# Transposing x once: the first stage stores its transposed tokens, the third stage completes them with an accumulating transfer

## The chip, the cores and the metric

The kernel runs on one core of one Trainium2 chip. The metric is device time in microseconds (us) of the whole program, all in float32. A core has TensorE (matmul, PE in the profile), VectorE (DVE), ScalarE (ACT), GpSimd (POOL) and SyncE (SP, which here only issues transfers), and 16 DMA engines that carry out the transfers of all of them.

## The reference

The input x has 384 x 384 tokens of 128 channels. Two layers follow each other, both on this array; all weights are 128 x 128.

```python
# layer 0
z = layernorm(x) * norm_g + norm_b
left  = (z @ Wl + bl) * sigmoid(z @ Wlg + blg)
right = (z @ Wr + br) * sigmoid(z @ Wrg + brg)
core = einsum('ikh,jkh->ijh', left, right)
x1 = x + sigmoid(x @ Wg + bg) * (layernorm(core) * onorm_g + onorm_b) @ Wout + bout-terms
# layer 1
left = x1 @ (W_left + W_eq) + biases
right_sum = sum over j of (x1 @ W_right + b_right)
out = (left * right_sum * sigmoid(x1 @ W_gate + b_gate)) @ W_out + b_out
y = layernorm(out + x1)
```

The layer norms take mean and variance over the 128 channels of a token. The sum over k in `core` needs every token of layer 0 before any token of the output, which splits the kernel into stages.

## The kernel before, in words

**First stage (0 to about 1142 us).** It walks over 144 chunks: 128 values of k on the partitions, eight values of i (XR), 128 channels. A chunk is two steps of four tokens per partition. `load_chunk` brings x (L106). `stats` computes mean and variance on VectorE (L215, L217), six steps ahead. `powers` turns them into rs = (var + eps)^-0.5 and sh = 1 - mean * rs on GpSimd (L224 to L227). `scale` writes z = x * rs + sh, the normalized token plus one, on GpSimd (L235). The "plus one" lets the bias of the weights come in by the matmul: the columns of `wz` are made so that the added one gives the bias. `front` transposes four tokens on TensorE (L244) and copies them to SBUF as zt (L246). `back` multiplies zt with the 512 columns of `wz` (left, right and the two gates, L267), applies the sigmoid on ScalarE (L269, two tokens at once) and the product on VectorE (L271) into the tile lr. A lr tile gathers 64 values of i (16 steps). It is written to DRAM (`lr_d`) by `store_slice` in eight slices of 1 MB (L253), one per step, during the 16 steps that fill the next tile. There are 18 such groups; the last two stay in SBUF and are not stored.

Per step, TensorE has half of `back`, then the four transposes for the next step, then the other half. The order of the instructions on each engine is written out by hand (`seq` keeps it); what an instruction waits for follows from the tiles it uses. A pool with n buffers of a tile makes its n+1st use wait until the first is free. A transfer is issued by the engine named in the code and waits in that engine's order.

**Second stage (about 1142 to 1885 us).** For each of the 128 h it loads left and right (L86, L87), makes nine pairs of matmuls (L357) and writes `core` to DRAM (L371), with sums for the layer norm over h.

**Third stage (about 1885 us to the end).** One iteration of the loop over t works on one row i of 384 tokens, with the channels on the partitions. `front(f)` runs ahead of the rest, by 14 rows at first and later by two. It transposes x of row f (three transposes, L448, and a copy on ScalarE to xT, L450) and, for row f - 2, computes the gate of layer 0 from xT (L440, sigmoid L442). `scale_core` multiplies core with its inverse deviation on GpSimd (L464). `layer0` makes x1T: matmul L473, then two operations on VectorE (L474, L476, which adds xT). `gated_left` has L490, L491, L493, L495, `layer1` L502 and L503 (which transposes the row back to tokens), `stats1` and `norm1` the last layer norm, `last` scale and shift of it, and `store` writes four rows at once. x is loaded four rows at a time by `load_x` (L399), 16 rows ahead; `load_core` brings four rows of core (L404) and of the inverse deviation, sent to all 128 partitions alike (rt, L406), eight rows ahead. Four PSUM banks rotate among the matmul results pg, pxt, pr, pg2, pl and pq, four others hold py.

So x is transposed twice: in the first stage after the normalization, in the third stage as it is.

Of the kernel before, what the change touches and what calls it, by code (L numbers as in the profile page):

```python
# [8 lines left out]
F32 = mybir.dt.float32  # L9
AF = mybir.ActivationFunctionType  # L10
ALU = mybir.AluOpType
# [8 lines left out]
def triangle_then_gated_row_kernel(ctx: ExitStack, tc: tile.TileContext, a: dict, out: bass.AP):  # L20
# [6 lines left out]

    nc = tc.nc  # L30
    x = a["x"].rearrange("b i j c -> (b i) j c")
    y = out.rearrange("b i j c -> (b i) j c")
# [7 lines left out]
    KEEP = 2  # L40
    RG = 4
    A = 14

    cpool = ctx.enter_context(tc.tile_pool(name="const", bufs=1))
# [3 lines left out]
    rstd_d = dpool.tile([N, N], F32, name="rstd_d")  # L48

    def seq(ins):  # L50

        return tc.keep_in_program_order(ins)
# [21 lines left out]
    with ExitStack() as ctx2:  # L74
# [13 lines left out]
                loaded2[h] = t  # L88

        with tc.tile_pool(name="p1x", bufs=6, side="right") as xp, \  # L90
             tc.tile_pool(name="p1w", bufs=3, side="right") as wp, \
             tc.tile_pool(name="p1s", bufs=5, side="right") as sp, \
             tc.tile_pool(name="p1t", bufs=2, space=PSUM) as tps, \
             tc.tile_pool(name="p1p", bufs=3, space=PSUM) as pps:
            NQ = XR // 4
# [111 lines left out]
            def stats(n, q, half):  # L207

                if q == 0 and half == 0:
                    normed[n] = [sp.tile(s, F32, tag=t, name=t) for t, s in  # L210
                                 (("st", [P, XR, 6]), ("mv", [P, XR, 2]), ("rs", [P, XR]), ("sh", [P, XR]))]
                st, mv, rs, sh = normed[n]
                r0 = 4 * q + 2 * half
                for r in range(r0, r0 + 2):
                    seq(nc.vector.bn_stats(st[:, r, :], loaded[n][:, r, :]))  # L215
                for r in range(r0, r0 + 2):
                    seq(nc.vector.bn_aggr(mv[:, r, :], st[:, r, :]))  # L217

            def powers(n, q):


                if q == NQ - 1:
                    _, mv, rs, sh = normed[n]
                    seq(nc.gpsimd.tensor_scalar(rs, mv[:, :, 1], EPS, 1.0, ALU.add, ALU.mult))  # L224
                    seq(nc.gpsimd.tensor_tensor(rs, rs, mhalf[:, :XR], ALU.pow))
                    seq(nc.gpsimd.tensor_tensor(sh, mv[:, :, 0], rs, ALU.mult))
                    seq(nc.gpsimd.tensor_scalar(sh, sh, -1.0, 1.0, ALU.mult, ALU.add))  # L227

            def scale(n, q):

                xt, (_, _, rs, sh) = loaded[n], normed[n]
                z = wp.tile([P, 4, C], F32, tag="z", name="z")
                for r in range(4):
                    rr = 4 * q + r
                    seq(nc.gpsimd.tensor_scalar(  # L235
                        z[:, r, :], xt[:, rr, :], rs[:, rr:rr + 1], sh[:, rr:rr + 1], ALU.mult, ALU.add
                    ))
                return z

            def front(z):  # L240
# [6 lines left out]
                return zt  # L247

            def store_slice():

# [5 lines left out]
                        in_=t[:, hs:hs + HS].rearrange("k h i s -> k h (i s)"),  # L256
                    ))

            def back(n, q, zt, half):

                kb, ig, c = chunks[n]
                if c == 0 and q == 0 and half == 0:
                    lr[kb, ig] = lrp.tile([P, H, G, 2], F32, tag="lr", name="lr")
                t = lr[kb, ig]
                pr = pps.tile([P, 2, 4 * H], F32, tag="pr", name="pr")
                for r in range(2):
                    seq(nc.tensor.matmul(pr[:, r, :], lhsT=zt[:, 2 * half + r, :], rhs=wz, start=True, stop=True))  # L267
                sg = wp.tile([P, 2, 2 * H], F32, tag="sg", name="sg")
                seq(nc.scalar.activation(sg, pr[:, :, 2 * H:], AF.Sigmoid))  # L269
                i0 = c * XR + 4 * q + 2 * half  # L270
                seq(nc.vector.tensor_tensor(  # L271
                    t[:, :, i0:i0 + 2, :],
                    pr[:, :, :2 * H].rearrange("k i (h s) -> k h i s", s=2),
                    sg.rearrange("k i (h s) -> k h i s", s=2),
                    ALU.mult,
                ))
# [7 lines left out]
            zs = {}  # L284
            for k in range(AHEAD):
                for half in range(2):
                    stats(*steps[k], half)
                if k == 1:
                    fold()
                if k == 2:  # L290
                    weights()
                if k < AHEAD - 1:
                    powers(*steps[k])
                if k == 1:
                    zs = {j: scale(*steps[j]) for j in range(2)}
                    zt = front(zs.pop(0))
            for k, (n, q) in enumerate(steps):
                ahead = None
                if k + 2 < len(steps):
                    zs[k + 2] = scale(*steps[k + 2])  # L300
                if k + AHEAD - 1 < len(steps):
                    powers(*steps[k + AHEAD - 1])
                for half in range(2):
                    back(n, q, zt, half)
                    if half == 0 and k + 1 < len(steps):
                        ahead = front(zs.pop(k + 1))
                    if k + AHEAD < len(steps):
                        stats(*steps[k + AHEAD], half)
                zt = ahead
                if q == NQ - 1:  # L310
                    del loaded[n], normed[n]
                    load_chunk(n + 6)
                store_slice()
                if k == 4:
                    for t, src in later:
                        load(t, src)
                if k == 20:
                    late_weights()
                if k == len(steps) - 2 * G // 4 + 16:
                    assert not full  # L320
                    for h in range(3):
                        load_h(h)
# [54 lines left out]
    with ExitStack() as ctx3:  # L377
        def pool(name, bufs, **kw):
            return ctx3.enter_context(tc.tile_pool(name=name, bufs=bufs, reuse_waits="tile", **kw))

        xip, fp, inp, op = pool("p3x", 4), pool("p3f", A + 4), pool("p3in", 3), pool("p3out", 3)
        wp, lp, sp = pool("p3w", 4), pool("p3l", 7), pool("p3s", 4)
        ps, ps2 = pool("p3ps", 4, space=PSUM), pool("p3ps2", 4, space=PSUM)

        def bank(name):
# [8 lines left out]
        rows, yts, pair, quad, xin, cin = {}, {}, {}, {}, {}, {}  # L394

        def load_x(i0):
            if i0 < N:
                xt = xin[i0] = xip.tile([P, RG, NB, C], F32, tag="xt", name="xt")
                seq(nc.sync.dma_start(out=xt, in_=x[i0:i0 + RG].rearrange("i (b p) c -> p i b c", p=P)))  # L399

        def load_core(i0):
            if i0 < N:
# [32 lines left out]
        def front(f):  # L435
# [5 lines left out]
                gT = r["gT"] = work("gT", fp)  # L441
                seq(nc.scalar.activation(gT, pg[:, :N], AF.Sigmoid, bias=bg0))  # L442
            if f < N:
                if f % RG == 0:
                    load_x(f + 4 * RG)
                pxt = bank("pxt")
                for b, s in enumerate(cols):
                    seq(nc.tensor.transpose(pxt[:, s], xin[f // RG * RG][:, f % RG, b, :], ident))  # L448
                xT = work("xT", fp)
                seq(nc.scalar.copy(xT, pxt[:, :N]))  # L450
                rows[f] = {"xT": xT}

        def right_sums(m):
# [12 lines left out]
        def layer0(i):  # L466
# [5 lines left out]
            pr = bank("pr")  # L472
            seq(nc.tensor.matmul(pr[:, :N], lhsT=wc, rhs=r["cs"], start=True, stop=True))  # L473
            seq(nc.vector.scalar_tensor_tensor(pr[:, :N], pr[:, :N], bz, r["gT"], ALU.add, ALU.mult))  # L474
            x1T = r["x1T"] = work("x1T", lp)
# [10 lines left out]
        def gated_left(i):  # L486
# [7 lines left out]
            u = r["u"] = work("u", lp)  # L494
# [54 lines left out]

        for i0 in range(0, 4 * RG, RG):  # L550
            load_x(i0)
        f = 0
        for t in range(N + 3):

            while f < min(N + 2, t + max(2, A - t // 3)):
                if f == 6:
                    rstd()
                    load_core(0)
# [72 lines left out]
```

## Time and profile before

The median of three runs is 3442.92 us (3438.89 to 3443.39); the profiled run has a span of 3438.5 us and a mean granted TensorE clock of 0.996.

| | first stage, 500 to 900 us | second stage, 1420 to 1600 us | third stage, 2400 to 2800 us |
|---|---|---|---|
| PE busy | 400.00 of 400 us | 180.00 of 180 us | 400.00 of 400 us |
| DVE busy | 268.71 | 94.62 | 329.07 |
| ACT busy | 173.20 | 70.75 | 306.48 |
| POOL busy | 293.62 | 105.43 | 291.75 |
| DMA share | 0.69 | 0.92 | 0.61 |
| GB/s | 196 | 283 | 198 |

Busy time is the time in which an engine has an instruction in work; the ends of matmuls are modelled. The DMA share is the mean busy share of the 16 DMA engines; it can exceed 1 in a short window, since an engine can have more than one packet in work. A line of groups reads: line, engine, operation, output <- inputs, shapes, count | busy us, mean ns of one | idle time of the engine just before them and what ended it.

Durations of one instruction that matter for what is changed: the transposes L448 and L244 274 ns (128x128), the copy L450 475 ns (128x384), the copy L246 580 ns (128x512), L235 448 ns (128x128), L474 and L476 625 and 618 ns (128x384). Transfers: a slice of lr is 1024 KB and lands 9.7 us (median) after its issue, a load of x in the first stage 512 KB and 7.7 us, a load of x in the third stage 768 KB and 4.9 us, one of rt 768 KB and 7.8 us.

### The profile page before, as it was taken

What the parts mean: (1) busy time and instruction counts of PE and PEld (TensorE: products, weight loads), DVE (VectorE), ACT (ScalarE), POOL (GpSimd) and SP (SyncE); (2) the same over time, 40 slices, a digit from 0 to 9 for tenths busy, and PEclk for the clock granted to TensorE, in tenths of its full rate; (3) what the DMA queues carried; (4) which work ended last, traced back from release to release, by engine and by line L of the source; (5) the groups of instructions that cost most, each with busy time, mean ns of one, the idle gap of its engine ahead of it and who ended that gap; (6) DMA issues with size and microseconds to landing.
All of it is one profiled execution on the core that took longest, in us unless ns stands there. A gap on an engine that the chain in (4) does not pass through costs nothing.

```text
span 3438.5 us, 48057 instructions
## 1 busy us (share of the span) xinstructions
PE 3398.4 (99%) x13646; PEld 2104.5 (61%) x13646; DVE 2414.3 (70%) x7498; ACT 1946.0 (57%) x3815; POOL 2357.5 (69%) x4041
## 2 busy tenths in 40 slices
PE   8999999999999999999999999999999999999998
PEld 4444444444444566666665677777777777777775
DVE  6666666666666555555555788888888888888887
ACT  3344444444444333333334677777777777777776
POOL 6677777777777455555655577777777777777776
PEclk9999999999999999999999999999999999999999
DMA  4776867758765599999999665665656666565662
GB/s 109 202 214 178 232 190 202 227 166 229 199 192 157 175 284 285 284 281 282 282 284 276 209 215 193 202 203 191 213 185 209 196 199 206 188 213 188 206 215 85
DMA packets 884865, 726.00 MB, mean 211 GB/s; under 512 B 18533, under 2 KB 823017, under 8 KB 884601
## 3 DMA queue, kind: packets, MB, share of 16 engines
q1 hardware_dynamic: 878176, 718.22, 67.9%
q10 hardware_dynamic: 6232, 4.13, 0.4%
q8 instruction: 110, 1.80, 0.2%
q14 instruction: 155, 1.26, 0.1%
q0 software_dynamic: 192, 0.59, 0.0%
HBM read 437.07 MB, written 285.80 MB: 210 GB/s over the span
## 4 chain that ended last, share of the span: by engine, by line
PE 98%; ACT 1%; DVE 0%; issue 0%; POOL 0%; DMA 0%; POOLq 0%; SPq 0%; ACTq 0%; DVEq 0%
PE pr L267 29%; PE pc L357 22%; PE pr L473 7%; PE py L502 7%; PE pg L440 7%; PE pg L490 7%; PE pl L491 7%; PE pt L244 4%; PE pxt L448 4%; PE py L503 4%; ACT py L533 0%; PE pq L457 0%; DMA xt<-in_x_dram 0%; POOL rs L522 0%; ACT gT L442 0%
## 5 line engine op out<-in xcount | busy, mean ns | idle before, releaser
L267 PE MATMUL pr<-wz,zt 128*128 128x512 f32 x2304 | 1040.0, 594 | 0.7 <-ACT zt L246 0.7
L357 PE MATMUL pc<-rr,lrh 128*128 128x384 f32 x2304 | 743.3, 486 | 1.5 <-issue 1.5
L269 ACT ACTIVATE sg<-pr 128x512 f32<-128x512 f32 x576 | 344.2, 598 | 644.9 <-PE pr L267 331.6
L267 PEld LDWEIGHTS pr<-wz,zt 128*128 128x128 f32 x2304 | 416.3, 191 | 414.9 <-issue 413.8
L271 DVE TENSOR_TENSOR lr<-pr,sg 128x512 f32<-128x512 f32 x576 | 398.5, 692 | 376.1 <-ACT sg L269 376.1
L357 PEld LDWEIGHTS pc<-rr,lrh 128*128 128x128 f32 x2304 | 451.8, 196 | 293.2 <-issue 2.3
L533 ACT ACTIVATE py<-py,nm,rs 128x128 f32<-128x128 f32 x1152 | 495.2, 430 | 120.2 <-POOL rs L526 89.8
L235 POOL TENSOR_SCALAR z<-xt,rs,sh 128x128 f32<-128x128 f32 x1152 | 497.7, 448 | 0.6 <-POOL z L235 0.4
L502 PEld LDWEIGHTS py<-wo,u 128*128 128x128 f32 x2304 | 377.5, 191 | 102.4 <-ACT wo L484 1.7
L366 DVE TENSOR_TENSOR csum<-csum,ct 128x1152 f32<-128x1152 f32 x128 | 184.8, 1444 | 351.1 <-ACT ct L363 351.1
L502 PE MATMUL py<-wo,u 128*128 128x128 f32 x2304 | 403.0, 275 | 1.2 <-ACT wo L484 1.2
L363 ACT COPY ct<-pc 128x1152 f32<-128x1152 f32 x128 | 143.3, 1119 | 450.1 <-PE pc L357 450.1
L343 POOL COPY rr<-lrh 128x768 f32<-128x768 f32 x128 | 184.5, 1442 | 307.6 <-DMA lrh<-lr_d 294.3
L464 POOL TENSOR_TENSOR cs<-ct,rt 128x384 f32<-128x384 f32 x384 | 383.3, 999 | 7.3 <-PE pr L473 5.4
L545 POOL TENSOR_TENSOR yt<-yt,lnb 128x384 f32<-128x384 f32 x384 | 383.8, 1000 | 2.9 <-DVE yt L544 2.7
L517 DVE BATCH_NORM_STATS2 st<-py 128x6 f32<-128x128 f32 x1152 | 266.7, 287 | 110.9 <-PE py L503 110.9
L473 PE MATMUL pr<-cs,wc 128*128 128x384 f32 x768 | 319.3, 497 | 0.7 <-ACT xT L450 0.7
L440 PE MATMUL pg<-xT,mat_L_conv_Wg 128*128 128x384 f32 x768 | 313.7, 490 | 4.7 <-ACT xT L450 4.7
L474 DVE SCALAR_TENSOR_TENSOR pr<-pr,bz,gT 128x384 f32<-128x384 f32 x384 | 240.2, 625 | 110.3 <-PE pr L473 110.3
L493 ACT ACTIVATE g<-pg,col_L_conv_b_gate 128x384 f32<-128x384 f32 x384 | 223.1, 581 | 162.2 <-PE pg L490 162.1
L503 PE MATMUL py<-ident,x1T 128*128 128x128 f32 x1152 | 314.0, 273 | 0.0
L490 PE MATMUL pg<-x1T,mat_L_conv_W_gate 128*128 128x384 f32 x768 | 310.9, 487 | 2.0 <-ACT gT L442 1.4
(88 smaller groups left out, 5125.8 us busy)
## 6 DMA issues: line engine op xcount, KB each, us to landing
lr_d<-lr SPq DMA_DIRECT2D x128, 1024.0 KB, 9.7
lrh<-lr_d SPq DMA_DIRECT2D x128, 768.0 KB, 7.7
xt<-in_x_dram SPq DMA_DIRECT2D x96, 768.0 KB, 4.9
ct<-core_d SPq DMA_DIRECT2D x96, 768.0 KB, 6.6
rt<-rstd_d SPq DMA_DIRECT2D x96, 768.0 KB, 7.8
out_dram<-yt SPq DMA_DIRECT2D x95, 768.0 KB, 9.1
core_d<-ct SPq DMA_DIRECT2D x125, 576.0 KB, 8.7
xt<-in_x_dram SPq DMA_DIRECT2D x140, 512.0 KB, 7.7
```

The source lines that it names most:

```text
L235: seq(nc.gpsimd.tensor_scalar(z[:, r, :], xt[:, rr, :], rs[:, rr:rr + 1], sh[:, rr:rr + 1], ALU.mult, ALU.add))
L267: seq(nc.tensor.matmul(pr[:, r, :], lhsT=zt[:, 2 * half + r, :], rhs=wz, start=True, stop=True))
L271: seq(nc.vector.tensor_tensor(t[:, :, i0:i0 + 2, :], pr[:, :, :2 * H].rearrange("k i (h s) -> k h i s", s=2), sg.rearrange("k i (h s) -> k ...
L357: seq(nc.tensor.matmul(pc[:, ib, :N], lhsT=t[:, kb, ib * P:(ib + 1) * P, 0], rhs=rr[:, kb], start=(kb == 0), stop=(kb == NB - 1),))
L440: seq(nc.tensor.matmul(pg[:, :N], lhsT=wg0, rhs=r["xT"], start=True, stop=True))
L464: seq(nc.gpsimd.tensor_tensor(cs, ct[:, i % RG], rt[:, i % RG], ALU.mult))
L473: seq(nc.tensor.matmul(pr[:, :N], lhsT=wc, rhs=r["cs"], start=True, stop=True))
L490: seq(nc.tensor.matmul(pg2[:, :N], lhsT=wgate, rhs=r["x1T"], start=True, stop=True))
L502: seq(nc.tensor.matmul(py[:, s], lhsT=r["u"][:, s], rhs=r["wo"], start=True, stop=False))
L503: seq(nc.tensor.matmul(py[:, s], lhsT=r["x1T"][:, s], rhs=ident, start=False, stop=True, is_transpose=True))
L533: seq(nc.scalar.activation(py[:, s], py[:, s], AF.Identity, bias=nm[:, n, b:b + 1], scale=rs[:, n, b:b + 1]))
L545: seq(nc.gpsimd.tensor_tensor(yt, yt, lnbb, ALU.add))
```

## The change

The third stage is to get the transposed x from the first stage. The first stage transposes the token only after scaling it by rs, which can't be undone by an addition. So the scaling is moved behind the matmul: with sd = (var + eps) * rs (the deviation) and nd = mean - sd, the first stage transposes z = x - nd. Then z * rs is again the normalized token plus one, and since rs belongs to a token (a partition of the matmul's output) it is applied as a per-partition scale in the sigmoid and in the product, which therefore work on one token at a time. The transposed z goes to DRAM (`xt_d`) with one 256 KB store per step, and nd, transposed in 18 blocks, to `nd_d`. In the third stage, from row TR = 24 on, `load_x` sends nd to all partitions, and `add_x` adds the stored z to it by a transfer that accumulates (issued by GpSimd, eight rows ahead of `front`); the sum is xT. The first 24 rows are transposed as before.

The pools follow: z and sg have two buffers instead of three, zt has a pool of its own with four, x of the third stage seven tiles instead of four, and the pool of x1T and u is opened later, on the side that the second stage has given up.

```diff
 # first stage
-             tc.tile_pool(name="p1w", bufs=3, side="right") as wp, \
+             tc.tile_pool(name="p1w", bufs=2, side="right") as wp, \
+             tc.tile_pool(name="p1z", bufs=4, side="right") as ztp, \
+             tc.tile_pool(name="p1d", bufs=2, side="right") as dp, \
...
-                    seq(nc.gpsimd.tensor_scalar(rs, mv[:, :, 1], EPS, 1.0, ALU.add, ALU.mult))
-                    seq(nc.gpsimd.tensor_tensor(rs, rs, mhalf[:, :XR], ALU.pow))
-                    seq(nc.gpsimd.tensor_tensor(sh, mv[:, :, 0], rs, ALU.mult))
-                    seq(nc.gpsimd.tensor_scalar(sh, sh, -1.0, 1.0, ALU.mult, ALU.add))
+                    seq(nc.gpsimd.tensor_scalar(sd, mv[:, :, 1], EPS, 1.0, ALU.add, ALU.mult))
+                    seq(nc.gpsimd.tensor_tensor(rs, sd, mhalf[:, :XR], ALU.pow))
+                    seq(nc.gpsimd.tensor_tensor(sd, sd, rs, ALU.mult))
+                    seq(nc.gpsimd.tensor_tensor(nd, mv[:, :, 0], sd, ALU.subtract))
...
-                        z[:, r, :], xt[:, rr, :], rs[:, rr:rr + 1], sh[:, rr:rr + 1], ALU.mult, ALU.add
+                    seq(nc.gpsimd.tensor_scalar(z[:, r, :], loaded[n][:, rr, :], nd, None, ALU.subtract))
...
-                zt = wp.tile([P, 4, P], F32, tag="zt", name="zt")
+                zt = zts[n, q] = ztp.tile([P, 4, P], F32, tag="zt", name="zt")
                 seq(nc.scalar.copy(zt, pt))
+            def store_zt(n, q):
+                kb, ig, c = chunks[n]
+                i0 = ig * G + c * XR + 4 * q
+                seq(nc.sync.dma_start(out=xt_d[:, i0:i0 + 4, kb, :], in_=zts.pop((n, q))))
+
+            def store_nd(kb, ig):
+                pt = tps.tile([P, 4, P], F32, tag="pt", name="pt")
+                seq(nc.tensor.transpose(pt[:G, 0], nds.pop((kb, ig)), ident))
+                ndt = dp.tile([G, P], F32, tag="ndt", name="ndt")
+                seq(nc.scalar.copy(ndt, pt[:G, 0]))
+                seq(nc.sync.dma_start(out=nd_d[ig * G:(ig + 1) * G, kb * P:(kb + 1) * P], in_=ndt))
...
-                seq(nc.scalar.activation(sg, pr[:, :, 2 * H:], AF.Sigmoid))
-                i0 = c * XR + 4 * q + 2 * half
-                seq(nc.vector.tensor_tensor(
-                    t[:, :, i0:i0 + 2, :],
-                    pr[:, :, :2 * H].rearrange("k i (h s) -> k h i s", s=2),
-                    sg.rearrange("k i (h s) -> k h i s", s=2),
-                    ALU.mult,
-                ))
+                for r in range(2):
+                    rr = 4 * q + 2 * half + r
+                    rs = normed[n][2][:, rr:rr + 1]
+                    seq(nc.scalar.activation(sg[:, r], pr[:, r, 2 * H:], AF.Sigmoid, scale=rs))
+                    seq(nc.vector.scalar_tensor_tensor(
+                        t[:, :, c * XR + rr, :],
+                        pr[:, r, :2 * H].rearrange("k (h s) -> k h s", s=2),
+                        rs,
+                        sg[:, r].rearrange("k (h s) -> k h s", s=2),
+                        ALU.mult, ALU.mult,
+                    ))
...
                 if q == NQ - 1:
                     del loaded[n], normed[n]
                     load_chunk(n + 6)
+                    if chunks[n][2] == G // XR - 1:
+                        store_nd(*chunks[n][:2])
+                store_zt(n, q)
                 store_slice()
 # third stage
+        def load_x(i0):
+            if i0 < TR:
...
+            elif i0 < N:
+                xt = xts[i0] = xp.tile([P, RG, N], F32, tag="xt", name="xt")
+                seq(nc.sync.dma_start(
+                    out=xt.rearrange("p i j -> p (i j)"),
+                    in_=nd_d[i0:i0 + RG].rearrange("i j -> (i j)").partition_broadcast(P),
+                ))
+
+        def add_x(i0):
+            if TR <= i0 < N:
+                seq(nc.gpsimd.dma_start(
+                    out=xts[i0].rearrange("p i j -> p (i j)"),
+                    in_=xt_d[:, i0:i0 + RG].rearrange("c i b k -> c (i b k)"), accum_op=ALU.add,
+                ))
...
+                if f >= TR:
+                    xT = xts[i0][:, n]
+                else:
+                    xT = work("xT", fp)
...
             if t % RG == 0:
                 load_core(t + 2 * RG)
+            if added <= f + 8:
+                add_x(added)
+                added += RG
             if t < N:
                 scale_core(t)
```

More of the change, by code (lines that the diff above doesn't have):

```diff
@@ L42, in triangle_then_gated_row_kernel @@
     A = 14
+    TR = 24
     cpool = ctx.enter_context(tc.tile_pool(name="const", bufs=1))
@@ L48, in triangle_then_gated_row_kernel @@
     rstd_d = dpool.tile([N, N], F32, name="rstd_d")
+    xt_d = dpool.tile([C, N, NB, P], F32, name="xt_d")
+    nd_d = dpool.tile([N, N], F32, name="nd_d")
     def seq(ins):
@@ L210, in stats @@
                     normed[n] = [sp.tile(s, F32, tag=t, name=t) for t, s in
-                                 (("st", [P, XR, 6]), ("mv", [P, XR, 2]), ("rs", [P, XR]), ("sh", [P, XR]))]
-                st, mv, rs, sh = normed[n]
+                                 (("st", [P, XR, 6]), ("mv", [P, XR, 2]), ("rs", [P, XR]), ("sd", [P, XR]))]
+                st, mv, _, _ = normed[n]
                 r0 = 4 * q + 2 * half
@@ L222, in powers, with shift @@
                 if q == NQ - 1:
-                    _, mv, rs, sh = normed[n]
-                    seq(nc.gpsimd.tensor_scalar(rs, mv[:, :, 1], EPS, 1.0, ALU.add, ALU.mult))
-                    seq(nc.gpsimd.tensor_tensor(rs, rs, mhalf[:, :XR], ALU.pow))
-                    seq(nc.gpsimd.tensor_tensor(sh, mv[:, :, 0], rs, ALU.mult))
-                    seq(nc.gpsimd.tensor_scalar(sh, sh, -1.0, 1.0, ALU.mult, ALU.add))
-            def scale(n, q):
-                xt, (_, _, rs, sh) = loaded[n], normed[n]
+                    _, mv, rs, sd = normed[n]
+                    kb, ig, c = chunks[n]
+                    if c == 0:
+                        nds[kb, ig] = dp.tile([P, G], F32, tag="nd", name="nd")
+                    nd = nds[kb, ig][:, c * XR:(c + 1) * XR]
+                    seq(nc.gpsimd.tensor_scalar(sd, mv[:, :, 1], EPS, 1.0, ALU.add, ALU.mult))
+                    seq(nc.gpsimd.tensor_tensor(rs, sd, mhalf[:, :XR], ALU.pow))
+                    seq(nc.gpsimd.tensor_tensor(sd, sd, rs, ALU.mult))
+                    seq(nc.gpsimd.tensor_tensor(nd, mv[:, :, 0], sd, ALU.subtract))
+            def shift(n, q):
+                kb, ig, c = chunks[n]
                 z = wp.tile([P, 4, C], F32, tag="z", name="z")
@@ L234, in scale, with front @@
                     rr = 4 * q + r
-                    seq(nc.gpsimd.tensor_scalar(
-                        z[:, r, :], xt[:, rr, :], rs[:, rr:rr + 1], sh[:, rr:rr + 1], ALU.mult, ALU.add
-                    ))
+                    nd = nds[kb, ig][:, c * XR + rr:c * XR + rr + 1]
+                    seq(nc.gpsimd.tensor_scalar(z[:, r, :], loaded[n][:, rr, :], nd, None, ALU.subtract))
                 return z
-            def front(z):
+            def front(n, q, z):
                 pt = tps.tile([P, 4, P], F32, tag="pt", name="pt")
@@ L244, in front @@
                     seq(nc.tensor.transpose(pt[:, r, :], z[:, r, :], ident))
-                zt = wp.tile([P, 4, P], F32, tag="zt", name="zt")
+                zt = zts[n, q] = ztp.tile([P, 4, P], F32, tag="zt", name="zt")
                 seq(nc.scalar.copy(zt, pt))
-                return zt
+            def store_zt(n, q):
+                kb, ig, c = chunks[n]
+                i0 = ig * G + c * XR + 4 * q
[6 more added lines that the diff above has]
+                seq(nc.sync.dma_start(out=nd_d[ig * G:(ig + 1) * G, kb * P:(kb + 1) * P], in_=ndt))
             def store_slice():
@@ L257, in store_slice, with back @@
                     ))
-            def back(n, q, zt, half):
+            def back(n, q, half):
                 kb, ig, c = chunks[n]
@@ L266, in back @@
                 for r in range(2):
-                    seq(nc.tensor.matmul(pr[:, r, :], lhsT=zt[:, 2 * half + r, :], rhs=wz, start=True, stop=True))
+                    seq(nc.tensor.matmul(
+                        pr[:, r, :], lhsT=zts[n, q][:, 2 * half + r, :], rhs=wz, start=True, stop=True
+                    ))
                 sg = wp.tile([P, 2, 2 * H], F32, tag="sg", name="sg")
-                seq(nc.scalar.activation(sg, pr[:, :, 2 * H:], AF.Sigmoid))
-                i0 = c * XR + 4 * q + 2 * half
-                seq(nc.vector.tensor_tensor(
-                    t[:, :, i0:i0 + 2, :],
-                    pr[:, :, :2 * H].rearrange("k i (h s) -> k h i s", s=2),
-                    sg.rearrange("k i (h s) -> k h i s", s=2),
-                    ALU.mult,
-                ))
+                for r in range(2):
[9 more added lines that the diff above has]
+                    ))
                 if c == G // XR - 1 and q == NQ - 1 and half == 1:
@@ L284, in triangle_then_gated_row_kernel @@
             zs = {}
+            nds, zts = {}, {}
             for k in range(AHEAD):
@@ L294, in triangle_then_gated_row_kernel @@
                 if k == 1:
-                    zs = {j: scale(*steps[j]) for j in range(2)}
-                    zt = front(zs.pop(0))
+                    zs = {j: shift(*steps[j]) for j in range(2)}
+                    front(*steps[0], zs.pop(0))
             for k, (n, q) in enumerate(steps):
-                ahead = None
                 if k + 2 < len(steps):
-                    zs[k + 2] = scale(*steps[k + 2])
+                    zs[k + 2] = shift(*steps[k + 2])
                 if k + AHEAD - 1 < len(steps):
@@ L303, in triangle_then_gated_row_kernel @@
                 for half in range(2):
-                    back(n, q, zt, half)
+                    back(n, q, half)
                     if half == 0 and k + 1 < len(steps):
-                        ahead = front(zs.pop(k + 1))
+                        front(*steps[k + 1], zs.pop(k + 1))
                     if k + AHEAD < len(steps):
                         stats(*steps[k + AHEAD], half)
-                zt = ahead
                 if q == NQ - 1:
@@ L379, in pool @@
             return ctx3.enter_context(tc.tile_pool(name=name, bufs=bufs, reuse_waits="tile", **kw))
-        xip, fp, inp, op = pool("p3x", 4), pool("p3f", A + 4), pool("p3in", 3), pool("p3out", 3)
-        wp, lp, sp = pool("p3w", 4), pool("p3l", 7), pool("p3s", 4)
+        xp, fp, inp, op = pool("p3x", 7), pool("p3f", A + 4), pool("p3in", 3), pool("p3out", 3)
+        wp, sp, late = pool("p3w", 4), pool("p3s", 4), []
         ps, ps2 = pool("p3ps", 4, space=PSUM), pool("p3ps2", 4, space=PSUM)
@@ L393, in triangle_then_gated_row_kernel @@
         lnbb = lnb.unsqueeze(1).to_broadcast([P, NB, C])
-        rows, yts, pair, quad, xin, cin = {}, {}, {}, {}, {}, {}
+        rows, yts, pair, quad, xin, xts, cin = {}, {}, {}, {}, {}, {}, {}
         def load_x(i0):
-            if i0 < N:
-                xt = xin[i0] = xip.tile([P, RG, NB, C], F32, tag="xt", name="xt")
-                seq(nc.sync.dma_start(out=xt, in_=x[i0:i0 + RG].rearrange("i (b p) c -> p i b c", p=P)))
+            if i0 < TR:
+                xt = xin[i0] = xp.tile([P, RG, N], F32, tag="xt", name="xn")
+                seq(nc.sync.dma_start(
+                    out=xt.rearrange("p i (b c) -> p i b c", b=NB),
+                    in_=x[i0:i0 + RG].rearrange("i (b p) c -> p i b c", p=P),
+                ))
+            elif i0 < N:
+                xt = xts[i0] = xp.tile([P, RG, N], F32, tag="xt", name="xt")
+                seq(nc.sync.dma_start(
+                    out=xt.rearrange("p i j -> p (i j)"),
+                    in_=nd_d[i0:i0 + RG].rearrange("i j -> (i j)").partition_broadcast(P),
+                ))
+        def add_x(i0):
[3 more added lines that the diff above has]
+                    in_=xt_d[:, i0:i0 + RG].rearrange("c i b k -> c (i b k)"), accum_op=ALU.add,
+                ))
         def load_core(i0):
@@ L443, in front @@
             if f < N:
-                if f % RG == 0:
+                i0, n = f // RG * RG, f % RG
+                if n == 0:
                     load_x(f + 4 * RG)
[L446 to L450, printed above, removed]
+                if f >= TR:
+                    xT = xts[i0][:, n]
+                else:
+                    xT = work("xT", fp)
+                    pxt = bank("pxt")
+                    for s in cols:
+                        seq(nc.tensor.transpose(pxt[:, s], xin[i0][:, n, s], ident))
+                    seq(nc.scalar.copy(xT, pxt[:, :N]))
                 rows[f] = {"xT": xT}
@@ L474, in layer0 @@
             seq(nc.vector.scalar_tensor_tensor(pr[:, :N], pr[:, :N], bz, r["gT"], ALU.add, ALU.mult))
-            x1T = r["x1T"] = work("x1T", lp)
+            x1T = r["x1T"] = work("x1T", late[0])
             seq(nc.vector.scalar_tensor_tensor(
@@ L493, in gated_left @@
             seq(nc.scalar.activation(g2, pg2[:, :N], AF.Sigmoid, bias=bgate))
-            u = r["u"] = work("u", lp)
+            u = r["u"] = work("u", late[0])
             seq(nc.vector.scalar_tensor_tensor(u, pl[:, :N], bleft, g2, ALU.add, ALU.mult))
@@ L551, in triangle_then_gated_row_kernel @@
             load_x(i0)
-        f = 0
+        f, added = 0, TR
         for t in range(N + 3):
@@ L557, in triangle_then_gated_row_kernel @@
                     rstd()
+                    end2.close()
+                    late.append(pool("p3l", 7, side="right"))
                     load_core(0)
```

## The prediction, made before the changed kernel was run

> **What bounds the kernel now.** First the page, for the chain of work that ended last.
>
> ```profile
> PE 3398.4 (99%) x13646; PEld 2104.5 (61%) x13646; DVE 2414.3 (70%) x7498; ACT 1946.0 (57%) x3815; POOL 2357.5 (69%) x4041
> PE 98%; ACT 1%; DVE 0%; issue 0%; POOL 0%; DMA 0%; POOLq 0%; SPq 0%; ACTq 0%; DVEq 0%
> ```
>
> TensorE is the path from end to end, so a matmul taken away is time gained wherever the other engines and the transfers can follow. The timeline of one row in the third stage tells what the removed transposes hold (start, duration, engine, line):
>
> ```profile
> 2600.52 0.81 PE L440 MATMUL pg<-xT,mat_L_conv_Wg 128*128 128x384 f32 x2
> ...
> 2601.17 0.49 PE L448 MATMUL pxt<-ident,xt 128*128 128x128 f32 x3
> ...
> 2601.49 0.81 PE L473 MATMUL pr<-cs,wc 128*128 128x384 f32 x2
> ...
> 2604.43 0.81 PE L440 MATMUL pg<-xT,mat_L_conv_Wg 128*128 128x384 f32 x2
> ```
>
> Read starts, not durations, since matmuls overlap: a row lasts 2604.43 - 2600.52 = 3.91 us, and the three transposes hold 2601.49 - 2601.17 = 0.32 us of it.
>
> Next, the groups that the edit touches (busy us, mean ns):
>
> ```profile
> L269 ACT ACTIVATE sg<-pr 128x512 f32<-128x512 f32 x576 | 344.2, 598 | 644.9 <-PE pr L267 331.6
> L271 DVE TENSOR_TENSOR lr<-pr,sg 128x512 f32<-128x512 f32 x576 | 398.5, 692 | 376.1 <-ACT sg L269 376.1
> L448 PE MATMUL pxt<-ident,xt 128*128 128x128 f32 x1152 | 189.5, 274 | 0.9 <-ACT ct L363 0.9
> ```
>
> Then the transfers. The change adds 75 MB of stores to the first stage, so I cut a stretch of that stage into windows of one step (four tokens per partition, 3.87 us). Last columns: clock, DMA share, GB/s.
>
> ```profile
> 334.85:338.72 3.87, 3.87 (x13) 1.91 (x13) 2.60 (x12) 1.67 (x3) 1.97 (x5) 1.00 0.17 50
> 338.72:342.59 3.87, 3.87 (x13) 1.91 (x13) 2.60 (x12) 1.67 (x3) 3.70 (x9) 1.00 0.98 283
> 342.59:346.46 3.87, 3.87 (x13) 1.91 (x13) 2.60 (x12) 1.67 (x3) 1.97 (x5) 1.00 0.92 219
> 346.46:350.34 3.88, 3.88 (x13) 1.92 (x13) 2.61 (x12) 1.67 (x3) 3.71 (x9) 1.00 1.15 342
> ...
> 369.70:373.57 3.87, 3.87 (x13) 1.91 (x13) 2.60 (x12) 1.67 (x3) 3.70 (x9) 1.00 1.01 273
> 373.57:377.44 3.87, 3.87 (x13) 1.91 (x13) 2.60 (x12) 1.67 (x3) 1.96 (x5) 1.00 0.82 205
> 377.44:381.31 3.87, 3.87 (x13) 1.91 (x13) 2.60 (x12) 1.67 (x3) 3.70 (x9) 1.00 0.00 0
> ```
>
> The stage's mean DMA share of 0.7 hides this: in every 16 steps (62 us) the eight 1 MB slices of L253 fill the DMA engines for ten steps, then they idle. The nine windows from 338.72 to 373.57 average 304 GB/s, 319 without the first two.
>
> **What the Trainium skill says.** "DMA: Bandwidth & Descriptors", section "SWDGE vs HWDGE vs iDMA": an accumulating transfer can only be issued by GpSimd, whose software writes the descriptors. The only GpSimd transfers here, the three stores of L431, occupied it for 563 ns each (median). The same page, "Issuing engines are not separate DMA queues": transfers of all issuers share the same 16 engines; no overlap of two busy queues is in this trace. "Anatomy of one DMA" there: about 2 us of each transfer is fixed, most of it the write receipt. That agrees: the fastest 512 KB load of x landed after 3.9 us, of which 0.52 MB at 304 GB/s are 1.7. "Collectives: The Full Stack", section "The bandwidth ceiling: the fold count and why AG ≠ RS ≠ AR": a reduce costs double because it reads two sources. No run here shows an accumulate yet.
>
> **Third stage, removed.** Rows from TR = 24 on lose the transposes: 360 x 0.32 = 115 us of TensorE, and 360 copies of L450 (475 ns) on ScalarE. For the row to shrink to 3.58 us, the others must fit. The window 2604.43 to 2608.33 has VectorE busy 3.22 us, unchanged by the edit: 90% of the new row. That is tight, but results are used an iteration or more later. ScalarE goes from 3.0 to about 2.55. I give back 2 us for lost overlap: gain 113.
>
> **Third stage, added.** GpSimd issues one accumulate per four rows: 0.56 to 1.0 us in 14.3, beside a mean busy 2.89 us per row, so at most 3.14 of 3.58. It waits there for the row-constant's load, issued eight rows (28 us) earlier, against 7.8 us for the same kind of load (rt); cs, yt and the powers queue behind it, but the wait is over by then. The sum has ten rows (35 us) before L440 wants it. Bytes: four transfers of 0.79 MB per four rows take about 9.2 us in the busy windows at 350 GB/s. The broadcast takes the place of the x load, the accumulate adds 2.25 us if it runs like a copy, 4.5 with two reads: 13.7 us of 14.3 at worst. I take 4.5; it fits, barely.
>
> **First stage, compute.** Per step TensorE does the same; 18 small transposes for the number per token add about 3 us with their weight loads. GpSimd has as many operations as before. The sigmoid splits from two of 598 ns to four of 128x256; between L533 (128x128 with scale and bias from memory, 430) and L269 (598) I take 490: +0.76 us on ScalarE's 1.67 of 3.87. VectorE's two 692 become four scalar_tensor_tensor; from L157 (128x512, 748) and L190 (128x128, 347) a 128x256 is 481: +0.54 on 2.60, so 3.14 of 3.87. Both are hidden by TensorE.
>
> **First stage, the store of zt.** This is where I expect loss. Each step adds 0.26 MB on the same SP queue. zt has four buffers, so the copy for step k+4 on ScalarE waits until the store of step k has landed; the sigmoids queue behind that copy, and TensorE's next step needs it. Work it out for the worst step of a burst. Count from the step boundary after which the first slice may go: the first slice was issued 2.0 us after it, bytes flowed about 3.0 after it. The eighth slice is queued ahead of the zt of step 7. Ahead of and with that zt go 8 slices (8.39 MB), 4 loads of x (2.10) and 8 zt (2.10): 12.6 MB. At 304 to 306 GB/s 41.2 us, plus 1.7 for the receipt: landed at 45.9. The copy and its signal, 0.7: zt of step 11 is ready at 46.6. TensorE wants it at 11 x 3.872 = 42.6. Stall 4.0 us per burst, once, since the later zt follow at 0.26 MB each. There are 18 groups, two of them kept: 16 bursts, 64 us. Ends for the rate: at 340 GB/s (the best windows) 0.4 us per burst, 6 in all; at 290, 6.2 and 99. Loads of x have seven steps of room, the lr buffer eight: hidden.
>
> **Sum.** 3443 - 113 + 3 + 64 = 3397; I say 3395.
>
> **Rivals.** (B) The stores are hidden after all: mixed reads and writes run at 340, or several zt land out of order. For it, the windows at 342; against it, the two slow windows at the head of every burst. Then 3443 - 113 + 3 + 0 to 6: 3335. (C) First stage slower: stores are dearer than loads, as the windows with slices alone (283, 219) hint, and the mean falls to 275. Then 12.6 MB last 45.8 us, stall 8.6, 137 in all: 3470, slower than before. (D) The accumulate runs at a third of a copy: 9.2 + 6.7 = 15.9 us per four rows, 3.98 per row, TensorE waits for transfers: +27 where I book -113, with the first stage's 67: 3537, slower. Nothing in the profile prices it; two reads speak for half the rate, not a third. (E) VectorE at 90% becomes the bound of the third stage with a row of about 3.7: gain 74, total 3436. Against it, it never waits on its own results within a row.
>
> **How the numbers follow.** Forecast 0.46, B 0.26, C 0.12, D 0.07, E 0.09. B and the forecast are faster; E splits between faster and the same; C and D are slower. Faster 0.79, same 0.04, slower 0.17. The range starts under B (3325) and ends at 3455, short of C and D.
>
> **What would show it.** After the change: pxt only for 24 rows and a row of 3.58 us in the third stage (else D or E: DMA share near 1, or VectorE without idle time). In the first stage, once per 16 steps, ScalarE's copy zt waiting for a DMA for some us, TensorE idle with it; none of that is B. It is wrong if steps outside bursts grow beyond 3.87 us (then the compute estimates fell), or if the accumulate holds GpSimd for many us.

## The result and the profile after

The changed kernel takes 3462.51 us (median; 3461.82 to 3463.03) against 3443.15 (3438.89 to 3443.7) for the kernel before on the same chip: a ratio of 1.0059, with a 95% interval of 1.0041 to 1.0076. It is slower by 19 us (0.6%) where 48 us less were forecast. The third stage did what it should; the first stage lost more than that.

The page of the changed kernel, busy times and the chain that ended last:

```profile
PE 3363.2 (97%) x12584; PEld 1986.6 (57%) x12584; DVE 2528.3 (73%) x8074; ACT 2014.3 (58%) x4049; POOL 2627.0 (76%) x4131
PE 85%; DMA 6%; ACT 3%; DVE 3%; POOL 1%; issue 1%; ACTq 0%; POOLq 0%; SPq 0%; DVEq 0%
```

TensorE had 98% of the chain and has 85%. What took its place is spread over DMA, ScalarE and VectorE: not one new bound, but a loop among engines that TensorE now waits for, and transfers.

Where the time went follows from when TensorE changes from one stage to the next. The first matmul of the second stage starts at 1273.2 us, before at 1142.2: the first stage is 131 us longer. The second is unchanged. From the last matmul of the second stage to the end it is 3460.0 - 2016.0 = 1444.0 us, before 3438.5 - 1885.0 = 1553.5: the third stage is 109.5 us shorter. The balance is +21.5 us of span.

The third stage first. The timeline of TensorE (start, duration, engine, line), from one gate matmul to the next:

```profile
2602.19 0.81 PE L489 MATMUL pg<-xt,mat_L_conv_Wg 128*128 128x384 f32 x2
2602.84 0.81 PE L526 MATMUL pr<-cs,wc 128*128 128x384 f32 x2
...
2605.77 0.81 PE L489 MATMUL pg<-xt,mat_L_conv_Wg 128*128 128x384 f32 x2
```

No transpose stands between pg and pr any more, and the row takes 2605.77 - 2602.19 = 3.58 us.

Now the first stage. The groups whose counts doubled, and the copy zt (busy us, mean ns | idle before, released by):

```profile
L298 ACT ACTIVATE sg<-pr,rs 128x256 f32<-128x256 f32 x1152 | 546.7, 475 | 534.0 <-DVE lr L299 326.7
L299 DVE SCALAR_TENSOR_TENSOR lr<-pr,rs,sg 128x256 f32<-128x256 f32 x1152 | 550.8, 478 | 376.2 <-ACT sg L298 368.5
```

The durations, 475 and 478 ns, are near what was reckoned with (490 and 481). The right-hand side is what counts: the sigmoid waits for the product, 327 us in all, and the product for the sigmoid, 369 us. Before, the profile names no product among what ended a sigmoid's wait (331.6 us ended by pr, 313.3 put down to VectorE's statistics). The timeline of half a step shows how it reaches TensorE:

```profile
408.64 0.47 ACT L298 ACTIVATE sg<-pr,rs 128x256 f32<-128x256 f32 x1 [0.73 <-PE pr L291]
...
409.15 0.48 DVE L299 SCALAR_TENSOR_TENSOR lr<-pr,rs,sg 128x256 f32<-128x256 f32 x1
...
409.67 0.47 ACT L298 ACTIVATE sg<-pr,rs 128x256 f32<-128x256 f32 x1 [0.55 <-DVE lr L299]
...
410.04 0.58 ACT L257 COPY zt<-pt 128x512 f32<-128x512 f32 x1
...
410.67 0.30 PEld L291 LDWEIGHTS pr<-wz,zt 128*128 128x128 f32 x2 [0.80 <-ACT zt L257]
```

Read it downward: sigmoid of token 1, product of token 1, only then the sigmoid of token 2, behind it in ScalarE's order the copy zt, and TensorE's weight load waits for zt. The weight load mostly sits idle for 0.24 us; here it is 0.80.

The starts of the copies zt in the timeline give the steps (the groups from the third on):

| steps, us | outside bursts | a group of 16 steps |
|---|---|---|
| before | 3.87 throughout | 62.0 |
| changed | 4.11 and 4.16 in turn | 68.5 to 71.8 while slices of lr are stored, mean 69.8 |

The bursts come on top of the longer step. Windows of 4 us through one burst (PE busy in the second place; granted clock, DMA share and GB/s last):

```profile
392.00:396.00 4.00, 4.00 (x13) 1.83 (x12) 2.88 (x13) 2.13 (x5) 2.82 (x6) 1.00 1.12 333
404.00:408.00 4.00, 3.14 (x8) 1.12 (x8) 2.31 (x11) 2.05 (x5) 3.36 (x6) 1.00 1.13 339
412.00:416.00 4.00, 2.81 (x10) 1.15 (x8) 2.56 (x11) 1.25 (x3) 2.24 (x4) 1.00 1.06 298
416.00:420.00 4.00, 3.15 (x8) 1.67 (x9) 1.58 (x6) 1.89 (x4) 2.37 (x5) 0.76 1.14 337
```

Late in the burst, with the DMA engines full, TensorE loses about a microsecond in a window (in the last one at a granted clock of 0.76; whether that costs anything besides the wait was not tried), and ScalarE's copy waits for a transfer (over the whole run: us in total, times, longest):

```profile
ACT zt L257 <- DMA xt_d<-zt: 37.0, 30, 2.6
```

### The profile page after: what moved, and what is told of

Same layout as the page of the kernel before. It is cut to its first block, busy times and chain, and to the rows that moved or that the text cites. A ratio compares the mean times of both kernels' runs of the same rounds, so it can differ in the third digit from the quotient of the medians.

```text
span 3460.0 us, 48243 instructions
## 1 busy us (share of the span) xinstructions
PE 3363.2 (97%) x12584; PEld 1986.6 (57%) x12584; DVE 2528.3 (73%) x8074; ACT 2014.3 (58%) x4049; POOL 2627.0 (76%) x4131
## 3 DMA queue, kind: packets, MB, share of 16 engines
q0 software_dynamic: 13152, 71.37, 10.1%
## 4 chain that ended last, share of the span: by engine, by line
PE 85%; DMA 6%; ACT 3%; DVE 3%; POOL 1%; issue 1%; ACTq 0%; POOLq 0%; SPq 0%; DVEq 0%
PE pr L291 23%; PE pc L388 21%; PE pr L526 7%; PE py L555 7%; PE pg L489 7%; PE pl L544 7%; PE pg L543 7%; DMA xt_d<-zt 5%; PE py L556 3%; PE pt L255 3%; DVE lr L299 2%; ACT sg L298 1%; ACT zt L257 1%; ACT py L586 1%; DVE st L223 1%
## 5 line engine op out<-in xcount | busy, mean ns | idle before, releaser
L291 PE MATMUL pr<-wz,zt 128*128 128x512 f32 x2304 | 1120.3, 611 | 48.7 <-ACT zt L257 44.5
L298 ACT ACTIVATE sg<-pr,rs 128x256 f32<-128x256 f32 x1152 | 546.7, 475 | 534.0 <-DVE lr L299 326.7
L299 DVE SCALAR_TENSOR_TENSOR lr<-pr,rs,sg 128x256 f32<-128x256 f32 x1152 | 550.8, 478 | 376.2 <-ACT sg L298 368.5
L291 PEld LDWEIGHTS pr<-wz,zt 128*128 128x128 f32 x2304 | 395.5, 191 | 554.6 <-issue 281.3
L248 POOL TENSOR_SCALAR z<-xt,nd 128x128 f32<-128x128 f32 x1152 | 675.4, 606 | 31.5 <-issue 22.0
L517 POOL TENSOR_TENSOR cs<-ct,rt 128x384 f32<-128x384 f32 x384 | 406.7, 1063 | 3.2 <-PE pr L526 2.6
L598 POOL TENSOR_TENSOR yt<-yt,lnb 128x384 f32<-128x384 f32 x384 | 406.3, 1058 | 2.9 <-DVE yt L597 2.6
L544 PE MATMUL pl<-x1T,mat_L_conv_W_left 128*128 128x384 f32 x768 | 312.1, 488 | 1.5 <-ACT gT L491 1.5
L489 PE MATMUL pg<-xt,mat_L_conv_Wg 128*128 128x384 f32 x720 | 292.0, 487 | 0.0
```

The lines of the kernel that those rows point to most:

```text
L248: seq(nc.gpsimd.tensor_scalar(z[:, r, :], loaded[n][:, rr, :], nd, None, ALU.subtract))
L291: seq(nc.tensor.matmul(pr[:, r, :], lhsT=zts[n, q][:, 2 * half + r, :], rhs=wz, start=True, stop=True))
L298: seq(nc.scalar.activation(sg[:, r], pr[:, r, 2 * H:], AF.Sigmoid, scale=rs))
L299: seq(nc.vector.scalar_tensor_tensor(t[:, :, c * XR + rr, :], pr[:, r, :2 * H].rearrange("k (h s) -> k h s", s=2), rs, sg[:, r].rearrange( ...
L489: seq(nc.tensor.matmul(pg[:, :N], lhsT=wg0, rhs=r["xT"], start=True, stop=True))
```

## The experiments

Two losses were to be told apart, and each tied to its cause. Times below are medians, beside 3441 to 3443 us for the kernel before in the same runs.

**An own sg tile per token** (e1). My first theory was that the two tokens of a half share the tile sg, so that writing the second half of it waits until the first was read.

```diff
-                sg = wp.tile([P, 2, 2 * H], F32, tag="sg", name="sg")
                 for r in range(2):
+                    sg = wp.tile([P, 2 * H], F32, tag=f"sg{r}", name="sg")
...
```

> Edit: each token of a half step gets its own sg tile instead of one half of a shared one; nothing else. Theory A (the two tokens of a half share a tile, so the second sigmoid waits until VectorE has read the first, the copy zt behind it comes late and TensorE waits for it): outside the bursts of stores the step falls from 4.14 us to 3.87, the wait of ScalarE for VectorE's lr (327 us in the changed kernel) goes away. In the burst groups the end of the transfers, not the step, sets the time, so most of the gain is eaten there: about 22 us over 16 burst groups and 8 over the other two, total 3430 (3385 if the stalls at the bursts don't grow). Rival B (the smaller operations are simply too much for ScalarE and VectorE, or the wait is for the matmul's tile): step stays near 4.14 us, total 3462.

Measured: 3463.26 us, steps still 4.11 and 4.16. From 100 to 1000 us of the trace:

```profile
ACT sg L298 <- DVE lr L299: 232.7, 407, 0.9
```

The changed kernel has 233.1 us there. The theory fell: sg is not what the second sigmoid waits for.

**lr stored in 16 slices** (e2), and **both edits** (e3).

```diff
-            HS = H // 8
+            HS = H // 16
```

> Edit: lr is stored in 16 slices of 512 KB over 16 steps instead of eight of 1 MB over eight; nothing else. Theory A (besides the longer step, the burst of stores delays the store of zt so that its buffer is not free in time: 3.5 us per burst, some 55 us in all): the groups of 16 steps fall from about 69.8 us to 66.2, ScalarE's wait of 37 us for the zt transfer goes, total 3407. Rival (DMA engines are too slow on average in the first stage): nothing gained, total about 3460.

> Both edits: own sg tile per token and 16 slices of lr. Theory A: the two losses are all there is, groups of 16 steps back at 62 us, first stage some 131 us shorter than in the changed kernel, total 3331 to 3340. If GpSimd, whose subtraction takes 606 ns where the scaling took 448, becomes the bound (about 7.2 us of work per two steps of 7.74): up to 20 us more.

Measured: 3415.35 us for e2, 47 less than the changed kernel; every group from the third on now takes 66.4 to 66.7 us, and the wait of ScalarE for the zt transfer is gone. So the bursts cost 47 us in the changed kernel. e3 gave 3414.42 where 3331 to 3340 was expected: the same, since its other edit does nothing.

**The computation without the stores** (e4). TR = 384, and the calls of `store_zt` and `store_nd` taken out.

```diff
-    TR = 24
+    TR = N
...
-                    if chunks[n][2] == G // XR - 1:
-                        store_nd(*chunks[n][:2])
-                store_zt(n, q)
```

> Edit: the first stage computes as in the changed kernel, but stores neither zt nor the number per token, and the third stage transposes x in all rows as before. This separates the compute of the first stage from its transfers. Theory A: step 4.11 us throughout, no stall at bursts, third stage as before the change: 3443 + 288 x 0.24 = 3512 to 3520. Rival (all of the first stage's loss comes with the transfers): 3443 to 3450.

Measured: 3523.9 us, groups of 66.3 us, third stage 3522.0 - 1967.0 = 1555.0 us as before the change. So 80.5 us are the price of computing per token, without any added transfer. The three parts add up: 3443 + 80.5 (step) + 47 (bursts) - 109.5 (third stage) = 3461.

**A PSUM tile per token** (e5) and **sigmoids ahead of products** (e6), each with the 16 slices. The list of waits in the built program of the changed kernel has the second sigmoid of each half waiting for VectorE alone, not even for TensorE. What the two tokens still shared was the matmul's tile pr in PSUM.

```diff
-             tc.tile_pool(name="p1p", bufs=3, space=PSUM) as pps:
+             tc.tile_pool(name="p1p", bufs=6, space=PSUM) as pps:
...
-                pr = pps.tile([P, 2, 4 * H], F32, tag="pr", name="pr")
+                pr = [pps.tile([P, 4 * H], F32, tag="pr", name="pr") for _ in range(2)]
...
```

e6 leaves the tiles as they are and cuts the loop in two:

```diff
                     seq(nc.scalar.activation(sg[:, r], pr[:, r, 2 * H:], AF.Sigmoid, scale=rs))
+                for r in range(2):
+                    rr = 4 * q + 2 * half + r
+                    rs = normed[n][2][:, rr:rr + 1]
                     seq(nc.vector.scalar_tensor_tensor(
```

> On top of the 16 slices: each token of a half step gets its own PSUM tile pr (six of one bank instead of three of two); sg shared as in the changed kernel. Theory A2 (the second sigmoid waits for VectorE's product of the first token because the two tokens share the tile pr, whatever sg is): ScalarE's wait for lr goes, step 3.87 us, groups of 16 steps 62 us instead of 66.4, total 3415 - 18 x 4.4 = 3336. Rival B2 (ScalarE and VectorE, with operations cut in two, are too slow for the step): step stays above 4 us, total about 3415.

> On top of the 16 slices: both tiles shared as in the changed kernel, but both sigmoids of a half are written ahead of both products, so that no sigmoid can wait for a product of its own half. Theory A2: step 3.87 us, total 3336, as with the tile of its own. Rival B2: about 3415. Rival C2 (GpSimd, 7.2 us of work per two steps, becomes the bound): step 3.9 to 4.0, total 3345 to 3370.

Measured: 3331.03 and 3333.69 us, ratios to the kernel before 0.9679 (0.9664 to 0.9693) and 0.9686 (0.9672 to 0.9701). Groups take 62.1 us in both. The timeline of e5:

```profile
420.18 0.47 ACT L298 ACTIVATE sg<-pr,rs 128x256 f32<-128x256 f32 x1 [0.39 <-PE pr L291]
...
421.09 0.47 ACT L298 ACTIVATE sg<-pr,rs 128x256 f32<-128x256 f32 x1 [0.43 <-PE pr L291]
...
421.70 0.45 DVE L299 SCALAR_TENSOR_TENSOR lr<-pr,rs,sg 128x256 f32<-128x256 f32 x1
...
421.90 0.47 ACT L298 ACTIVATE sg<-pr,rs 128x256 f32<-128x256 f32 x1 [0.34 <-PE pr L291]
...
422.33 0.59 ACT L257 COPY zt<-pt 128x512 f32<-128x512 f32 x1
```

The sigmoids are paced by TensorE (0.81 to 0.91 us apart, with 1.03 in the changed kernel), the second sigmoid of a half (421.90) starts while the first token's product (421.70 to 422.15) still runs, and the copy follows at once. The operations are the same, as many and as long; only the tile differs, or the order. So the wait comes from the shared pr together with the order in which the operations were written, and from nothing that the engines can't do. e5 is 110 us below the kernel before; no kernel of the study is faster (e9 below has the same time within the scatter).

**GpSimd's subtraction.** L248 takes 606 ns where L235 took 448 (from start to start 582 and 429), which the prediction had not reckoned with. e7 (on e6) writes it with two operations, e9 (on e5) as multiply-add with both numbers read per partition.

```diff
-                    seq(nc.gpsimd.tensor_scalar(z[:, r, :], loaded[n][:, rr, :], nd, None, ALU.subtract))
+ e7:                seq(nc.gpsimd.tensor_scalar(z[:, r, :], loaded[n][:, rr, :], nd, 1.0, ALU.subtract, ALU.mult))
+ e9:                seq(nc.gpsimd.tensor_scalar(z[:, r, :], loaded[n][:, rr, :], one, sd, ALU.mult, ALU.add))
```

(In e9 `one` is a column of ones and sd holds -nd.)

> As the run before, and GpSimd's z = x - nd is written with two operations (minus nd, times 1.0). If the 606 ns of the changed kernel's L248 come from the form with one operation, it goes back to about 448 ns; if they come from VectorE's new operation beside it, it stays near 606. Total as the run before if GpSimd is not the bound, up to 20 us less if it is.

> On top of 16 slices and a PSUM tile per token: GpSimd makes z as x times one plus (-nd), multiply then add with both numbers read per partition, which is the form of the kernel before; one more 8-element operation per chunk gives -nd. If the pair of operations sets the duration (multiply-add 448 ns, subtract alone 602 to 606, subtract and multiply 717), z is back at 448 ns and GpSimd's busy share of the first stage falls from 0.89 to about 0.62 + 0.05; if the operands' addresses or the neighbours on VectorE set it, z stays near 600. The time stays at 3331 either way, since TensorE has the path.

Measured: 3400.17 us for e7, a miss both ways, and 3332.0 for e9. One line each of the views of z (count: minimum/median/maximum ns), e7 and then e9:

```profile
L248 POOL TENSOR_SCALAR z<-xt,nd x1152: 706/717/730, 10.5 to 1202.7; 128x128 f32<-128x128 f32 x192
```

```profile
L251 POOL TENSOR_SCALAR z<-xt,one,sd x1152: 443/448/476, 10.8 to 1131.3; 128x128 f32<-128x128 f32 x192
```

VectorE's operations are the same in e5 and e9, so the form of the operation sets the duration. e7 shows how little room GpSimd had: at 717 ns it is busy 380 of 400 us, a group takes 66.1 us, and GpSimd has become the bound: it has 29% of the chain that ended last, where the changed kernel has 1%. e9 gives it back a lot of room (303 of 400 us against 357 in e5) and no time, since TensorE has the path.

**The price of the addition** (e10, on e5): the same transfer without `accum_op`.

> On top of 16 slices and a PSUM tile per token: the third stage's GpSimd transfer copies the stored tokens instead of adding them (so the number per token is left out of x from row 24 on). It prices the addition: in the changed kernel one such transfer of 768 KB takes 3.75 us of all 16 engines (26.2% of 400 us for 27.9 of them). If adding doubles the cost by its second read, the plain copy takes about 2.0 us and the DMA share of the third stage falls from 0.90 to about 0.78; the time stays at 3331, since rows are paced by TensorE at 3.58 us. If the price is that of transfers issued by GpSimd, nothing falls.

Measured: 3333.36 us, one execution; this kernel leaves the number per token out of x. The queue of GpSimd's transfers over the whole run (packets, MB, share of 16 engines), changed kernel and e10:

```profile
q0 software_dynamic: 13152, 71.37, 10.1%
```

```profile
q0 software_dynamic: 13152, 71.37, 6.9%
```

With 90 transfers of 0.79 MB in each, 10.1% of 3460.0 us makes 3.88 us of all engines for an accumulating one, and 6.9% of 3331.6 us makes 2.55 for a copy. (The expectation's 3.75 is somewhat low: the 21.24 MB that passed from 2400 to 2800 us are 27.0 transfers, not 27.9.) Adding costs 1.5 copies, not two, and the DMA share of the stage falls from 0.90 to 0.80 with no effect on the time: between 2400 and 2800 us TensorE is busy 400 us in both.

The addition shows on GpSimd too. One of its products of the third stage in the changed kernel and in e10, and one issue of an accumulating transfer in the changed kernel with the two products behind it:

```profile
L517 POOL TENSOR_TENSOR cs<-ct,rt 128x384 f32<-128x384 f32 x384 | 406.7, 1063 | 3.2 <-PE pr L526 2.6
```

```profile
L517 POOL TENSOR_TENSOR cs<-ct,rt 128x384 f32<-128x384 f32 x384 | 384.3, 1001 | 3.6 <-PE pr L526 1.2
```

```profile
2607.51 0.90 POOL L445 DMA_DIRECT2D xt<-xt_d  x1
2608.19 1.27 POOL L517 TENSOR_TENSOR cs<-ct,rt 128x384 f32<-128x384 f32 x1
2609.15 1.26 POOL L598 TENSOR_TENSOR yt<-yt,lnb 128x384 f32<-128x384 f32 x1
```

Behind an accumulating issue the two products are recorded with 1.26 us in the mean, all others with 1.00, and in e10, behind a plain copy's issue, with 1.01. But starts count here as well: the product starts 0.68 us after the issue (0.66 in e10), and the next one 0.96 us after that, in both kernels. The records overlap, and GpSimd loses next to nothing.

**The burst by itself** (e8, e11). e8 is the changed kernel with the loop cut in two and its slices of 1 MB: the step and the bursts that the prediction had reckoned with. e11 adds two buffers of zt, for one of x.

```diff
-        with tc.tile_pool(name="p1x", bufs=6, side="right") as xp, \
+        with tc.tile_pool(name="p1x", bufs=5, side="right") as xp, \
...
-             tc.tile_pool(name="p1z", bufs=4, side="right") as ztp, \
+             tc.tile_pool(name="p1z", bufs=6, side="right") as ztp, \
```

> The changed kernel with its eight slices of 1 MB, only the sigmoids written ahead of the products. This is the kernel that the prediction reckoned with (step 3.87 us, bursts as they are). By the prediction's sum (64 us of stalls at bursts): 3397. If the end of a burst is set by the transfers alone, as in the run with an own sg tile, the shorter step is eaten by longer stalls in 16 of 18 groups: 3430.

> The kernel with its eight slices of 1 MB and the sigmoids ahead of the products (3425.6 us), with six buffers of zt instead of four; to make room in SBUF x has five buffers instead of six. If the stalls at bursts come from zt's buffers not being free in time, two more steps of room (7.7 us) exceed the stall of 5.9 us per burst and nearly all of it goes: 3334 to 3345. If the transfers of a burst are too much for the DMA engines however deep the queue is, the time stays near 3425. If the loads of x, now with one buffer less, come late, VectorE's statistics wait for them and the time is between.

Measured: 3425.55 us (3417.58 to 3431.55) for e8. Its burst groups take 68.0 us in the mean, 5.9 more than without a burst, and 1.8 less than the changed kernel's at its longer step: of the 4.3 us by which a group without a burst is shorter, most is spent waiting for the end of the transfers. e11: 3336.03 us, every group 62.1, with the same bytes in the same bursts. So the transfers fit, even with one buffer of x less; what was missing was time between a store's issue and the next use of its buffer. Deeper buffers or smoother stores cure it alike.

## Why the prediction was wrong

The step that failed is "First stage, compute": sigmoids and products split in two were costed by busy time, 2.43 and 3.14 us of 3.87, and the prediction concludes "Both are hidden by TensorE". The durations were right and the conclusion false. The edit also put a product between two sigmoids of one PSUM tile, and the second sigmoid waits for it; the copy zt stands behind it, and TensorE behind the copy. That is 0.24 to 0.29 us per step that no busy time shows, 80.5 us in all (e4), and it goes without any operation made shorter (e5, e6). No rival held this. Rival C's total, 3470, came nearest by luck: its reason, stores at 275 GB/s, is not what the traces show (294 in a burst of e8, below). The prediction's last paragraph named the sign, steps outside the bursts longer than 3.87 us, and that is what appeared.

The other steps:

- *Third stage, removed*: right. 113 us forecast, 109.5 measured, a row of 3.58 us. VectorE at 88% (352 of 400 us) did not bind, so rival E fell.
- *Third stage, added*: right, with room to spare. 4.5 us were booked for the accumulate, 3.88 measured (as a copy 2.25, measured 2.55; the 9.2 us for the four other transfers at 350 GB/s should read 9.0). Issuing it takes GpSimd 0.90 us by the record, and 0.68 from its start to that of the next operation; it waited for its nd once, 5.3 us. Rival D fell. The Trainium skill's reason, a second read ("Collectives: The Full Stack", "The bandwidth ceiling: the fold count and why AG ≠ RS ≠ AR"), gives a factor of two for the reduce of a collective; here it is 1.5.
- *The store of zt*: the mechanism was right, as e2 and e11 show, except that the stall does not come once per burst. One burst of e8:

```profile
383.83 0.58 ACT L257 COPY zt<-pt 128x512 f32<-128x512 f32 x1 [1.55 <-DMA xt_d<-zt]
...
392.94 0.59 ACT L257 COPY zt<-pt 128x512 f32<-128x512 f32 x1 [1.60 <-DMA xt_d<-zt]
...
403.78 0.59 ACT L257 COPY zt<-pt 128x512 f32<-128x512 f32 x1 [3.33 <-DMA xt_d<-zt]
```

The size: 4.0 us per burst and 64 in all were reckoned for a step of 3.87; in e8, which has that step, it is 5.9, and e8 less e6 is 92 us. The mis-sized term is the time for the 12.6 MB. The burst above moved 294 GB/s (358.46 to 401.16 us) where 304 to 306 were taken; at 294 the prediction's sum gives 42.8 us for the bytes and a stall of 5.6, if its start and receipt were right (the receipt's 1.7 us was taken from no trace). One end of the range is off too: at 340 GB/s the sum leaves no stall, not 0.4 us. In the changed kernel the longer step hides part of the bursts, 47 us are left. Rival B fell.
- *18 small transposes*: 3 us forecast; the step that holds one is 0.11 us longer (3.98 against 3.87 in e5), 2 us.
- *GpSimd has as many operations as before*: true, but each subtraction is 158 ns longer. It cost nothing here, as e9 beside e5 shows; GpSimd had 11% left (357 of 400 us busy in e5).

Without the bursts the forecast's terms, as measured, give 3443 - 109.5 + 2 = 3335.5, and e6 has 3333.69. With the 92 us of the bursts it is 3427.5, and e8, the kernel that the prediction describes, has 3425.55 (no second check, since the 92 come from it). The changed kernel had the step loss besides.

## What to carry to other kernels

When an operation is split so that two engines alternate on one tile, write down who waits for whom before adding up busy times: the wait falls on whatever is queued behind the waiting operation, and an engine can be the one that TensorE waits for though it is busy little more than half of the time (ScalarE: 219 of 400 us in the changed first stage). Give each part a tile of its own, or let one engine finish all its parts before the next begins. And where transfers come in bursts, compare the time that a buffer has until its next use with the length of the burst, not the average rate with the peak: two more buffers or half-size slices were worth 90 us here without a byte less.

## What the hardware showed that was not expected

- GpSimd's tensor_scalar on 128x128 float32: multiply-add with two per-partition numbers 448 ns, subtract alone 602 to 608, subtract and multiply by a constant 717 (from start to start 429, 579 to 582 and 694). That the pair of operations is the reason, and not that a number is constant or absent, was not tried apart.
- A GpSimd transfer of 768 KB that adds into SBUF took 3.88 us of all 16 DMA engines, a copy 2.55; their issues are recorded with 905 and 634 ns.
- ScalarE and VectorE, which read different halves of one PSUM tile, were put in sequence by the program's waits; with a tile for each half they ran beside each other (e5, 421.90 us).
- GpSimd's two products (128x384) right behind the issue of an accumulating transfer are recorded with 1.26 us, the others with 1.00, though they start 0.96 us apart in both cases; without the addition (e10) the difference is gone. Why the records are longer is open.
